# Two graph-network layers on one core: the score block in two PSUM tiles, and a new written-out order of all engines

## The chip, the core and the metric

The kernel runs on one core of a Trainium2 chip. The metric is device time in microseconds (us). A core has five engines that matter here, each with its own queue, which it works through in order: TensorE (PE: matrix products, with its weight loads shown as PEld), VectorE (DVE), ScalarE (ACT), GpSimd (POOL) and SyncE (SP), which here issues all transfers between HBM and the on-chip memory SBUF. TensorE writes its results to PSUM, a small memory of eight banks, from which DVE and ACT read; POOL works in SBUF alone.

## The reference

There are 64 graphs of 256 nodes with 256 features each, and for each graph an integer adjacency matrix. Two layers are applied one after the other; everything is float32. Cut to what matters:

```
# layer 0: 8 heads of 32; four relations r, of which this adjacency has values 0 and 1
q, k = x @ Wq + bq, x @ Wk + bk                    # split in heads
attn = softmax(q @ k.T / sqrt(32))
out  = sum over r of (attn * (adj == r)) @ (x @ Wv[r] + bv[r])
x    = layernorm(x + out @ Wo + bo)
x    = layernorm(x + gelu(x @ W1 + b1) @ W2 + b2)

# layer 1: 8 heads of 32
e    = leaky_relu(q @ k.T, 0.2)
attn = softmax(e where adj > 0, else -9e15)
h    = layernorm(attn @ v)
out  = layernorm(concat(h, x) @ Wffn.T) + x
```

## The kernel before

The function fast_path (line 232) treats graph after graph. For each one, program(g) (line 310) makes a list of operations, each with a name, the engine that runs it, and a function that emits its instructions. A name carries the layer and the group of four heads: q0, k0 and v0 are the queries, keys and values of layer 0; s01 is the score block of layer 0, head group 1; e and m are the exponentials (m the masked ones in layer 0, the positive part in layer 1); es is the sum of the two halves of e; po is the product with the values, with the row sums beside it; rd is the reciprocal of the row sums; o is their product; py is a transposition, y0, y1 and y2 are normalised rows; ph and pw2 are the two products of the feed-forward part; ph and pwa (without a number) belong to the end of layer 1. A suffix like /1 is the pair of heads inside a group, and #2 the second operation on the same name.

A score block (score, line 428) is eight matmuls of 32 rows: two halves of the keys, four heads each. Four heads use four strips of rows of the array at once. The products po (weighted, line 462) use four strips of columns at once. All other matmuls use the whole array. So TensorE changes between three forms: full array, row tiles (s) and column tiles (po).

All 1,024 scores per partition and pair of heads are read from PSUM twice. In layer 0, ACT takes exponentials (exps, line 443) and DVE adds a large negative number where the adjacency has an edge (without_edges, line 452); ACT then takes exponentials of that too, and POOL adds halves (halves_added, line 495). In layer 1, DVE adds the mask, ACT takes the positive part (emit_positive, line 704), POOL adds both (emit_leaky, line 708), and ACT takes exponentials of the sum.

PSUM is shared out by the table TAGS (line 58): "s" has one buffer of four banks, which holds a whole score block, and "g" has four buffers of one bank each for everything else, used in turn. When a tile has been read for the last time, its buffer can be written anew. Waits are put in by the framework from what reads and writes which tile. Buffers in SBUF are in the same table; e and m have three each.

The order is not left to the framework. in_order (line 45) gives each operation the time g x PERIOD + STARTS[name] and sorts all operations of all graphs by it; they are emitted in that order, so each engine's queue follows it. The times in STARTS (line 100) only rank; the period that the chip shows is another. The first four graphs and the last four have lists of their own, FIRST (line 120) and LAST (line 177), with one number for each operation. Graph 0 also has the fetches of the weights (fetch, line 510) and two small products, pbf and pmean (lines 553 and 564), which turn the last weight matrix wf into a scaled and centred one: pbf needs the operation "wide" (from the columns) and the fetched wf, then DVE copies and scales (emit_scaled, line 559), then pmean follows.

For one period in the middle of the run the order before is, on TensorE, with the graph relative to the newest one in brackets:

```
pk1[-2] pq1[-2] po00[-1] po01[-1] s10[-2] pv1[-2] pwo[-1] pwb[-2] pk0[0] pq0[0] py0[-1] s11[-2]
ph6 ph0 ph2 ph4[-1] s00[0] po10[-2] pw2 x8[-1] s01[0] po11[-2] pva0[0] pva1[0] py1[-1] ph[-2] pwa[-2]
```

At the start it begins pq0 pk0 pva1 s00 pbf pva0 pmean s01 po00 po01 pwo (all graph 0), then pq0 of graph 1, py0, pk0 of graph 1, ph0. SP issues adj, wq0, rows0, xT, wk0, wv01, cols, wo, wfT, rows1, x, wv1, w1, w2, wk1, wq1. At the end, with graph numbers, it is: py0.63, ph.63 x4, po10.62, pw2.63 x8, po11.62, ph.62, py1.63, pwa.62, pk1, pq1, s10, pwb, pv1, s11, po10, po11, ph, pwa (all of 63).

Of the kernel before, what the change touches and what calls it, by code (L numbers as in the profile page):

```python
# [17 lines left out]
ALPHA = 0.2  # L18
# [26 lines left out]
def in_order(programs, starts, period, first, last):  # L45
# [4 lines left out]
    for g, p in enumerate(programs):  # L50
# [31 lines left out]
    "s": ([HPG, NT, D], F32, 1),  # L82
# [18 lines left out]
    "xT": 16.39, "x": 17.62, "pk0": 18.03, "adj": 19.67, "neg": 20.08, "pq0": 21.31, "k0": 22.13, "q0": 25.00,  # L101
    "s00": 31.15, "m00/1": 33.61, "e00/0": 37.30, "e00/1": 38.52, "m00/1#2": 39.34, "m00/0": 40.16, "s01": 40.57,
    "e01/0": 40.98, "e01/1": 41.39, "m00/0#2": 44.26, "pva0": 45.49, "es01/1": 46.31, "v0/0": 46.72, "pva1": 47.13,
    "v0/1": 48.36, "es00/0": 48.77, "es00/1": 50.82, "m01/0": 52.05, "m01/0#2": 52.87, "m01/1": 54.92,
    "es01/0": 55.33, "m01/1#2": 57.38, "po00": 57.79, "rd00": 58.20, "po01": 58.61, "o0/0": 60.25,
    "DVE:po01": 61.48, "rd01": 62.30, "o0/1": 62.70, "pwo": 63.11, "DVE:po00": 63.52, "res": 64.34, "pwo#2": 65.57,
    "mv0": 66.80, "rs0": 67.21, "y0": 69.26, "py0": 71.72, "y0T": 72.54, "ph6": 75.41, "ph0": 76.64, "hT/6": 77.87,
    "ph2": 78.69, "hT/2": 79.10, "ph4": 79.51, "hT/0": 79.92, "hT/4": 80.74, "pw2": 81.97, "pw2#2": 82.38,
    "r1": 82.79, "r1#2": 83.20, "pw2#3": 84.43, "pw2#4": 84.84, "pw2#5": 85.66, "pw2#6": 86.07, "pw2#7": 86.48,
    "pw2#8": 88.93, "pw2#9": 91.80, "mv1": 93.03, "rs1": 93.44, "y1": 94.67, "py1": 97.54, "y1T": 97.95,  # L110
    "pk1": 100.00, "ACT:adj": 100.41, "pq1": 104.10, "q1": 104.51, "k1": 109.02, "s10": 109.43, "m10/0": 109.84,
    "pv1": 110.66, "v1": 111.07, "x2": 111.89, "pwb": 113.93, "e10/0": 114.75, "e10/1": 115.16, "e10/0#2": 115.98,
    "m10/1": 118.44, "e10/1#2": 118.85, "e10/0#3": 120.49, "es10/0": 120.90, "zb": 122.95, "s11": 123.36,
    "e11/1": 123.77, "x2#2": 124.18, "e11/0": 124.59, "e10/1#3": 125.82, "es10/1": 126.23, "m11/0": 127.05,
    "m11/1": 127.46, "e11/1#2": 128.28, "e11/0#2": 130.33, "po10": 131.56, "rd10": 134.02, "o1/0": 135.25,
    "e11/1#3": 136.89, "e11/0#3": 137.70, "es11/0": 138.11, "es11/1": 139.75, "po11": 142.21, "DVE:po10": 142.62,
    "rd11": 143.85, "o1/1": 145.08, "DVE:po11": 145.90, "ph": 149.18, "pwa": 149.59, "mv2": 151.23, "rs2": 151.64,
    "pwa#2": 152.46, "mv3": 153.28, "rs3": 153.69, "y2": 155.74, "y2#2": 156.15, "y2#3": 156.56, "SP:y2": 156.97,
# [3 lines left out]
        -2847.053, -2618.669, -2552.639, -2604.994, -2706.544, -2524.281, -2429.355, -2491.963, -2326.15, -2291.878,  # L122
        -2205.017, -2453.681, -2501.433, -2475.116, -1979.242, -2495.418, -2281.166, -2149.469, -1954.32, -1950.672,
        -2629.93, -2490.837, -2900.007, -2402.608, -1755.256, -2397.873, -2429.046, -2408.233, -2387.015, -2337.739,
        -2248.383, -2096.592, -2381.743, -2040.963, -2323.494, -1986.344, -2170.731, -2048.634, -1860.558, -2191.888,
        -2201.038, -2121.273, -1987.509, -1858.163, -1687.597, -1539.069, -1758.675, -1901.191, -1868.775, -1849.204,
        -1797.723, -1842.922, -1866.564, -1901.189, -1864.039, -1710.05, -1635.372, -1608.525, -1601.055, -1611.923,
        -1504.663, -1503.313, -1503.311, -1454.211, -1453.749, -1428.651, -1397.418, -1365.689, -1263.132, -1333.428,
        -1307.057, -1302.867, -1269.069, -1279.736, -1246.049, -1318.829, -1287.58, -1268.965, -1234.872, -1196.915,
        -1176.186, -1166.684, -1155.815, -1135.153, -1127.66, -1127.658, -1125.664, -1116.163, -1109.387, -1096.892,  # L130
        -1068.525, -1058.771, -834.708, -1034.909, -1034.369, -1037.42, -971.802, -873.683, -861.526, -817.316,
        -794.117, -948.046, -931.884, -938.676, -839.591, -800.872, -786.885, -935.815, -938.986, -873.329, -822.37,
        -800.254, -703.594, -628.579, -521.145, -703.592, -852.402, -753.92, -797.646, -753.918, -687.087, -549.142,
        -801.786, -794.56, -679.67, -651.382, -613.255, -519.88, -503.788, -460.172, -508.16, -452.842, -406.466,
        -405.026, -445.465, -387.29, -386.804, -373.855, -368.241, -277.528, -258.371, -211.016,
    ],
    [
        -1712.66, -1443.453, -1558.578, -1409.383, -424.973, -1332.342, -1515.918, -1376.199, -1389.201, -1376.896,
        -1176.315, -1175.399, -1171.179, -1142.744, -1372.605, -1177.435, -1233.494, -1225.381, -1169.756, -1364.499,
        -1211.174, -1210.635, -1283.409, -1142.483, -1107.236, -1024.81, -1042.32, -1168.101, -1163.006, -1109.044,  # L140
        -1086.417, -1040.287, -1117.876, -1135.775, -1092.749, -1107.742, -1028.857, -1019.047, -1019.045, -962.29,
        -953.415, -933.383, -905.03, -894.712, -878.269, -878.267, -878.265, -878.267, -829.154, -849.496, -805.626,
        -860.667, -839.105, -834.236, -762.88, -849.583, -795.469, -753.483, -652.438, -623.714, -612.52, -604.112,
        -604.11, -604.108, -597.853, -597.851, -580.455, -541.025, -525.23, -510.162, -510.16, -234.294, 26.726,
        -461.818, -418.06, -444.927, -353.251, -347.025, -276.942, -284.894, -256.944, -353.249, -292.158, -353.247,
        -288.969, -272.27, -239.253, -352.105, -312.477, -253.791, -237.655, -177.565, -140.907, -63.211, -56.41,
        -132.185, -252.617, -248.041, -236.522, -133.806, -99.059, -66.449, -235.239, -211.498, -143.046, -63.735,
        -23.871, -15.497, 7.986, 8.437, -15.495, 28.391, 37.806, 44.002, 37.535, 66.321, 66.323, 87.244, 87.246,
        116.225, 189.089, 204.842,
    ],  # L150
    [
        -1229.881, -526.973, -1181.68, -1178.71, 66.635, -396.146, -1031.055, -966.68, -943.117, -935.039, -608.969,
        -560.147, -579.485, -523.949, -808.47, -704.853, -753.672, -752.036, -617.846, -650.977, -671.842, -631.081,
        -641.14, -494.019, -442.274, -439.507, -456.199, -629.154, -609.944, -493.554, -466.947, -559.795, -577.488,
        -482.336, -418.455, -494.253, -414.141, -410.734, -406.722, -370.63, -396.854, -333.908, -310.914, -309.856,
        -309.854, -305.407, -305.13, -200.379, -114.553, -302.188, -284.917, -285.604, -156.698, -263.97, -217.918,
        -280.388, -230.946, -154.247, -111.16, -83.43, -79.414, -74.774, -71.445, -70.202, -70.114, -67.694, -67.692,
        -67.69, -53.693, -53.691, -53.689, -24.507, 209.443, 29.562, 64.838, -35.526, 9.223, 71.488, 99.662, 113.468,
        120.616, 69.818, 89.502, 70.022, 89.536, 110.394, 124.527, 109.105, 79.783, 120.842, 123.12, 124.465, 131.394,
        133.646, 137.555, 133.656, 123.327, 128.611, 127.875, 129.152, 133.924, 133.926, 123.329, 127.217, 128.709,  # L160
        133.424, 138.627, 142.388, 142.522, 146.364, 145.361, 151.44, 151.442, 153.783, 152.66, 153.785, 153.787,
        155.037, 155.83, 196.784, 209.445, 209.447,
    ],
    [
        -394.579, -455.288, -369.201, -318.002, -85.508, -1.925, -382.842, -372.891, -372.581, -353.322, -106.738,
        -80.656, -102.13, -71.463, -265.115, -179.435, -120.231, -102.022, -128.718, -168.609, -153.486, -32.837,
        -58.709, -10.119, 11.78, 27.092, 37.379, -119.809, -73.356, -86.43, -39.705, -50.805, -93.331, -55.921,
        -14.902, -55.763, 4.094, 33.398, 33.4, 47.121, 58.796, 65.314, 65.316, 67.626, 72.399, 72.484, 72.486, 72.401,
        78.893, 74.741, 81.291, 76.79, 81.396, 75.033, 81.051, 79.917, 81.961, 83.124, 83.126, 84.564, 85.156, 88.277,
# [62 lines left out]
def fast_path(nc, tc, a, out, bad):  # L232
# [13 lines left out]
    with ExitStack() as ctx:  # L246
# [63 lines left out]
        def program(g):  # L310
# [117 lines left out]
            def score(q, k, hg, n):  # L428
                def emit():
                    s, qT, kT = T(f"s{n}{hg}"), T(q), T(k)  # L430
                    for c in range(NT):
                        for j in range(HPG):
# [3 lines left out]
                                start=True, stop=True,  # L436
                            )

                op("PE", [q, k], [f"s{n}{hg}:s"], emit)
                for t in ("e", "m", "es"):  # L440
                    tags[f"{t}{n}{hg}"] = t

# [625 lines left out]
```

## Time and profile before

| what | value |
|---|---|
| median of three runs | 2937.29 us (2935.6 to 2937.31) |
| the profiled execution: own time | 2934.98 us |
| its span, first to last instruction | 2932.8 us |
| TensorE busy | 2882.9 us (98%) |
| DVE / ACT / POOL busy | 1961.4 / 1788.6 / 2017.2 us |
| granted clock of TensorE | 0.995 |
| DMA moved | 76.65 MB, mean 26 GB/s |
| one period in the middle (two successive po00) | 44.79 us |

A profile comes from one execution. The page gives busy time by engine, the span in 40 slices (a digit is the busy share in tenths), the chain of work that ended last, and groups of instructions. A line of the timeline has the start, the time up to the end of the last instruction, the engine, the line of the kernel, the operation, what it writes and reads, the array's form and the shape, and how many instructions were merged; in square brackets, the idle time before it and what ended it. One fp32 matmul is two instructions. The ends of matmuls are modelled, so starts are the safer thing to take differences of.

### The profile page before, as it was taken

To read this page: it belongs to the slowest core of one execution; us is meant where nothing else is said; L and a number is where in the kernel's file an instruction comes from. 1 tells how busy PE (TensorE), PEld (TensorE's weight loads), DVE (VectorE), ACT (ScalarE), POOL (GpSimd) and SP (SyncE) were. 2 spreads that over 40 slices of the span, in tenths; PEclk is the share of its full clock that TensorE was granted. 3 is DMA by queue.
4 is the path that set the end of the run, shared out by engine and by line. 5 is a ranking of instruction groups with operands and counts; after the bars stand their busy time and mean duration, and the time that the engine had idled before them with its cause. 6 is when DMAs were issued, how large, how long until landed. Compare 5 with 4: busy or idle time off the path is not lost.

```text
span 2932.8 us, 53746 instructions
## 1 busy us (share of the span) xinstructions
PE 2882.9 (98%) x21770; PEld 2154.7 (73%) x21770; DVE 1961.4 (67%) x3668; ACT 1788.6 (61%) x3009; POOL 2017.2 (69%) x1542
## 2 busy tenths in 40 slices
PE   7999999999999999999999999999999999999996
PEld 5777777777777777777777777777777777777774
DVE  4676676676766766766767667667667676676674
ACT  4656656566566566566665665665666656656653
POOL 2657767767767667677667676676776676766666
PEclk9999999999999999999999999999999999999997
DMA  3000100000000000000000000000000000010000
GB/s 123 15 19 16 33 30 15 30 19 26 30 15 30 30 15 30 30 15 30 21 24 30 16 30 30 16 30 30 15 30 23 23 30 16 30 34 15 30 16 8
DMA packets 74331, 76.65 MB, mean 26 GB/s; under 512 B 4448, under 2 KB 73568, under 8 KB 74080
## 3 DMA queue, kind: packets, MB, share of 16 engines
q1 hardware_dynamic: 74080, 73.17, 7.8%
q8 instruction: 174, 2.85, 0.4%
q14 instruction: 77, 0.63, 0.1%
HBM read 56.37 MB, written 16.78 MB: 25 GB/s over the span
## 4 chain that ended last, share of the span: by engine, by line
PE 96%; DVE 1%; POOL 1%; ACT 1%; issue 1%; DMA 0%; SPq 0%; DVEq 0%; ACTq 0%; POOLq 0%
PE ph L658 15%; PE pw L676 15%; PE po L470 12%; PE s L434 9%; PE pva L610 8%; PE pq L338 8%; PE pk L338 7%; PE pv L352 4%; PE pwa L352 4%; PE po L475 4%; PE pwo L352 4%; PE pwb L352 4%; PE py L364 2%; PE ph L364 1%; POOL e L710 1%
## 5 line engine op out<-in xcount | busy, mean ns | idle before, releaser
L710 POOL TENSOR_TENSOR e<-e,m 128x1024 f32<-128x1024 f32 x256 | 601.3, 2359 | 231.7 <-DVE e L457 148.8
L501 POOL TENSOR_TENSOR es<-e 128x512 f32<-128x512 f32 x512 | 644.4, 1274 | 153.1 <-ACT e L448 143.1
L457 DVE TENSOR_TENSOR m<-s,neg 128x1024 f32<-128x1024 f32 x256 | 311.8, 1219 | 483.8 <-PE s L434 327.7
L484 DVE RECIPROCAL rd<-po 128x256 f32<-128x256 f32 x256 | 449.2, 1755 | 132.1 <-PE po L475 124.5
L410 POOL TENSOR_TENSOR rs<-ve,neg_half 128x2 f32<-128x2 f32 x256 | 178.5, 697 | 479.6 <-DVE ve L405 479.3
L706 ACT ACTIVATE m<-s 128x1024 f32<-128x1024 f32 x256 | 255.2, 1022 | 371.2 <-PE s L434 226.1
L658 PE MATMUL ph<-y0T,w 128*128 128x256 f32 x2048 | 459.2, 382 | 0.7 <-ACT y0T L380 0.7
L676 PE MATMUL pw<-w,hT 128*128 128x256 f32 x2048 | 459.0, 382 | 0.0
L676 PEld LDWEIGHTS pw<-w,hT 128*128 128x128 f32 x2048 | 383.9, 190 | 75.6 <-issue 25.1
L658 PEld LDWEIGHTS ph<-y0T,w 128*128 128x128 f32 x2048 | 383.8, 190 | 71.2 <-issue 20.6
L457 DVE TENSOR_TENSOR e<-s,neg 128x1024 f32<-128x1024 f32 x256 | 302.1, 1218 | 146.8 <-PE s L434 122.9
L448 ACT ACTIVATE e<-s 128x1024 f32<-128x1024 f32 x256 | 258.9, 1014 | 187.4 <-PE s L434 167.1
L448 ACT ACTIVATE m<-m 128x1024 f32<-128x1024 f32 x256 | 269.5, 1055 | 66.8 <-DVE m L457 66.8
L434 PE MATMUL s<-q,k 32*128 32x256 f32 x4096 | 293.3, 400 | 3.1 <-DVE e L457 1.4
L448 ACT ACTIVATE e<-e 128x1024 f32<-128x1024 f32 x256 | 270.4, 1056 | 27.1 <-POOL e L710 26.2
L470 PE MATMUL po<-e,v 128*32 128x256 f32 x4096 | 276.4, 385 | 4.3 <-ACT e L448 4.3
L434 PEld LDWEIGHTS s<-q,k 32*128 32x128 f32 x4096 | 185.1, 184 | 89.9 <-issue 78.7
L610 PE MATMUL pva<-wv,xT 128*128 128x512 f32 x512 | 237.0, 605 | 0.0
L470 PEld LDWEIGHTS po<-e,v 128*32 128x32 f32 x4096 | 114.1, 109 | 125.5 <-issue 45.4
L665 ACT ACTIVATE hT<-ph,cols 128x256 f32<-128x256 f32 x512 | 194.6, 488 | 3.4 <-PE ph L658 2.6
L610 PEld LDWEIGHTS pva<-wv,xT 128*128 128x128 f32 x512 | 92.1, 189 | 115.7 <-issue 115.4
L475 PE MATMUL po<-es,ones 128*32 128x256 f32 x2048 | 160.2, 381 | 4.0 <-POOL es L501 4.0
(90 smaller groups left out, 4546.5 us busy)
## 6 DMA issues: line engine op xcount, KB each, us to landing
adj<-adjT_dram SPq DMA_DIRECT2D x64, 256.0 KB, 3.6
xT<-xT_dram SPq DMA_DIRECT2D x64, 256.0 KB, 3.0
x<-x_dram SPq DMA_DIRECT2D x64, 256.0 KB, 3.1
out_dram<-y SPq DMA_DIRECT2D x64, 256.0 KB, 2.2
w<-L_gnn_W_dram SPq DMA_DIRECT2D x2, 1024.0 KB, 10.3
rows<-rows_dram SPq DMA_DIRECT2D x1, 896.0 KB, 7.4
wv<-L_gnn_Wv_dram SPq DMA_DIRECT2D x3, 256.0 KB, 7.2
wq<-L_gnn_Wq_dram SPq DMA_DIRECT2D x2, 256.0 KB, 5.9
```

The lines of the kernel that those rows point to most:

```text
L338: nc.tensor.matmul(pt[:, o, :], lhsT=w[:, c, o * P : (o + 1) * P], rhs=s[:, c, :], start=(c == 0), stop=(c == KC - 1),)
L352: nc.tensor.matmul(pt[:, t, :], lhsT=T(s)[:, c, t * P : (t + 1) * P], rhs=w, start=(n == 0), stop=(n == len(parts) - 1),)
L434: nc.tensor.matmul(s[:, j, c, :], lhsT=kT[r, hg, c * P : (c + 1) * P], rhs=qT[r, hg, :], start=True, stop=True,)
L448: nc.scalar.activation(T(dst)[:, j], T(src)[:, j], AF.Exp, scale=scale, **kw)
L457: lambda: nc.vector.tensor_tensor(T(dst)[:, j], T(src)[:, j], T("neg")[:, None].to_broadcast([P, 2, NT, D]), ALU.add),
L470: nc.tensor.matmul(po[j * DH : (j + 1) * DH, 0, :], lhsT=v(c, j), rhs=T(e)[:, j, c, :], start=(n == 0 and c == 0), stop=(n == len(parts) - ...
L484: op("DVE", [po], [f"{rd}:rd"], lambda: nc.vector.reciprocal(T(rd), T(po)[:, 1, :]))
L501: lambda: on.tensor_tensor(T(dst)[:, j], T(e)[:, j, 0, :], T(e)[:, j, 1, :], ALU.add),
L610: nc.tensor.matmul(pv.rearrange("p r d -> p (r d)"), lhsT=s[:, c, t * P : (t + 1) * P], rhs=wv0[:, c].rearrange("p r d -> p (r d)"), start ...
L658: nc.tensor.matmul(ph[:, i, :], lhsT=w1[:, c, (f + i) * P : (f + i + 1) * P], rhs=s[:, c, :], start=(c == 0), stop=(c == KC - 1),)
L676: nc.tensor.matmul(T("pw2")[:, t, :], lhsT=T("hT")[:, f + i, t * P : (t + 1) * P], rhs=w2[:, f + i, :], start=(f + i == 0), stop=(f + i == ...
L710: nc.gpsimd.tensor_tensor(T(f"e1{hg}")[:, j], T(f"e1{hg}")[:, j], T(f"m1{hg}")[:, j], ALU.add)
```

## The change

There are two parts. First, the score block is split: the tag "s" now has tiles of half the size and two of them, so a block has one tile for each pair of heads, and each reader names the tile of its pair. The eight matmuls are the same, in the same order, and write to one tile or the other. PSUM as a whole is used as before (two tiles of two banks in place of one of four).

Second, the tables STARTS, FIRST and LAST are new.

```diff
-    "s": ([HPG, NT, D], F32, 1),
+    "s": ([2, NT, D], F32, 2),
...
 def score
-                    s, qT, kT = T(f"s{n}{hg}"), T(q), T(k)
+                    s, qT, kT = [T(f"s{n}{hg}{pair}") for pair in range(2)], T(q), T(k)
                     for c in range(NT):
                         for j in range(HPG):
                             r = slice(j * DH, (j + 1) * DH)
                             nc.tensor.matmul(
-                                s[:, j, c, :], lhsT=kT[r, hg, c * P : (c + 1) * P], rhs=qT[r, hg, :],
+                                s[j // 2][:, j % 2, c, :], lhsT=kT[r, hg, c * P : (c + 1) * P], rhs=qT[r, hg, :],
                                 start=True, stop=True,
                             )
-                op("PE", [q, k], [f"s{n}{hg}:s"], emit)
+                op("PE", [q, k], [f"s{n}{hg}{pair}:s" for pair in range(2)], emit)
...
 def exps
-                    nc.scalar.activation(T(dst)[:, j], T(src)[:, j], AF.Exp, scale=scale, **kw)
-                op("ACT", [src if src.startswith("s") else f"{src}/{pair}"], [f"{dst}/{pair}"], emit)
+                    s = T(dst)[:, j] if src == dst else T(src)
+                    nc.scalar.activation(T(dst)[:, j], s, AF.Exp, scale=scale, **kw)
+                op("ACT", [f"{dst}/{pair}" if src == dst else src], [f"{dst}/{pair}"], emit)
...
 def without_edges
-                        T(dst)[:, j], T(src)[:, j], T("neg")[:, None].to_broadcast([P, 2, NT, D]), ALU.add
+                        T(dst)[:, j], T(src), T("neg")[:, None].to_broadcast([P, 2, NT, D]), ALU.add
...
-                    exps(f"s0{hg}", f"e0{hg}", SCALE, pair, 2 * hg + pair)
-                    without_edges(f"s0{hg}", f"m0{hg}", pair)
+                    exps(f"s0{hg}{pair}", f"e0{hg}", SCALE, pair, 2 * hg + pair)
+                    without_edges(f"s0{hg}{pair}", f"m0{hg}", pair)
...
-                    without_edges(f"s1{hg}", f"e1{hg}", pair)
+                    without_edges(f"s1{hg}{pair}", f"e1{hg}", pair)
-                        nc.scalar.activation(T(f"m1{hg}")[:, j], T(f"s1{hg}")[:, j], AF.Relu, scale=1.0 / ALPHA - 1.0)
+                        nc.scalar.activation(T(f"m1{hg}")[:, j], T(f"s1{hg}{pair}"), AF.Relu, scale=1.0 / ALPHA - 1.0)
-                    op("ACT", [f"s1{hg}"], [f"m1{hg}/{pair}"], emit_positive)
+                    op("ACT", [f"s1{hg}{pair}"], [f"m1{hg}/{pair}"], emit_positive)
```

The new STARTS (the old ones follow from the order shown above):

```diff
+    "xT": 47.54, "adj": 54.92, "neg": 55.74, "pq0": 56.97, "q0": 60.25, "pk0": 70.08, "k0": 70.90, "s000": 72.95,
+    "e00/0": 81.15, "m00/1": 81.56, "m00/0": 87.70, "e00/1": 90.98, "pva0": 93.44, "s010": 94.26, "v0/0": 95.08,
+    "e01/0": 96.72, "x": 97.13, "m00/1#2": 97.95, "pva1": 100.82, "res": 101.64, "e01/1": 102.05, "es00/1": 102.87,
+    "v0/1": 103.28, "es01/0": 104.10, "m00/0#2": 106.56, "m01/1": 107.38, "m01/1#2": 107.79, "m01/0": 108.61,
+    "m01/0#2": 109.43, "es00/0": 111.07, "po00": 111.48, "rd00": 112.30, "o0/0": 112.70, "es01/1": 113.11,
+    "po01": 114.34, "rd01": 114.75, "o0/1": 115.16, "DVE:po01": 115.57, "DVE:po00": 116.39, "ACT:adj": 118.44,
+    "pwo": 118.85, "pwo#2": 119.26, "mv0": 119.67, "rs0": 123.77, "y0": 124.18, "py0": 124.59, "y0T": 125.00,
+    "r1": 129.51, "ph0": 131.97, "ph4": 132.79, "hT/0": 134.43, "hT/4": 134.84, "ph2": 135.25, "hT/2": 135.66,
+    "ph6": 136.07, "hT/6": 136.48, "r1#2": 138.11, "pw2": 138.52, "pw2#2": 138.93, "pw2#3": 139.34, "pw2#4": 139.75,
+    "pw2#5": 140.16, "pw2#6": 140.57, "pw2#7": 141.39, "pw2#8": 141.80, "pw2#9": 142.21, "mv1": 142.62,
+    "rs1": 145.49, "y1": 145.90, "py1": 148.36, "y1T": 148.77, "pk1": 153.69, "pq1": 154.51, "k1": 155.33,
+    "q1": 158.20, "s100": 159.02, "e10/0": 159.84, "m10/0": 160.66, "e10/1": 161.89, "x2": 163.52, "m10/1": 163.93,
+    "s110": 165.98, "e11/0": 166.80, "m11/1": 167.21, "pv1": 167.62, "v1": 168.03, "m11/0": 170.49,
+    "e10/1#2": 171.31, "e11/1": 172.13, "pwb": 172.54, "e10/0#2": 173.36, "e11/0#2": 175.41, "zb": 176.64,
+    "e10/1#3": 177.05, "es10/1": 177.46, "e11/1#2": 182.38, "e10/0#3": 183.20, "e11/0#3": 183.61, "es10/0": 184.02,
+    "e11/1#3": 186.89, "es11/1": 193.03, "po10": 193.85, "es11/0": 194.67, "po11": 196.31, "rd10": 199.18,
+    "DVE:po11": 199.59, "o1/0": 200.00, "DVE:po10": 200.41, "rd11": 201.23, "o1/1": 202.46, "x2#2": 206.15,
+    "ph": 221.72, "mv2": 225.82, "rs2": 226.23, "pwa": 227.87, "pwa#2": 228.28, "mv3": 228.69, "rs3": 229.10,
+    "y2": 229.92, "y2#2": 230.33, "y2#3": 230.74, "SP:y2": 237.30,
...
```

Sorted, one period on TensorE now reads:

```
pva1[-1] pk1[-2] pq1[-2] pq0[0] s10[-2] po00[-1] po01[-1] s11[-2] pv1[-2] pwo[-1] pk0[0] ph[-3] pwb[-2] s00[0]
py0[-1] pwa[-3] ph0 ph4 ph2 ph6[-1] pw2 x8[-1] pva0[0] po10[-2] s01[0] po11[-2] py1[-1]
```

A graph's operations are now spread over some four periods where they took three, and the end of layer 1 (ph, pwa) runs one period later. FIRST and LAST (numbers left out) give these orders. At the start TensorE's queue is pbf pmean pq0 pk0 s00 pva1 s01 pva0 po00 po01 pwo (graph 0), pk0 and pq0 of graph 1, py0, s00 of graph 1, ph0 ph2 ph6 ph4, pw2 x8, pva1 and pva0 of graph 1, py1, s01 of graph 1, pk1. SP issues cols, wv01, wk0, xT, wfT, wq0, rows1, adj, rows0, x, w1, wv1, wo, wk1, w2, wq1. At the end: pwo.63, pwb.62, pv1.62, py0.63, pwa.61, ph0.63, ph4, ph2, the first pw2, ph6, the other seven pw2, po10.62, po11.62, py1.63, pq1, pk1, ph.62, s10.63, pv1.63, pwa.62, s11.63, pwb, po10, po11, ph, pwa (all of 63). There POOL has rs3.62, y2.62 and their like behind the last half sum es11/1.63, and DVE has y2.62 between o1/0.63 and rd11.63.

## The prediction

> **What bounds the kernel now.** I read the page first: which engine is full, and where it is not.
>
> ```profile
> span 2932.8 us, 53746 instructions
> ...
> PE 2882.9 (98%) x21770; PEld 2154.7 (73%) x21770; DVE 1961.4 (67%) x3668; ACT 1788.6 (61%) x3009; POOL 2017.2 (69%) x1542
> ...
> PE   7999999999999999999999999999999999999996
> ...
> PEclk9999999999999999999999999999999999999997
> ```
>
> TensorE is full in 38 slices of 40; only the first and last (73.3 us each) have room. Cut to 300-2700 us, the table of waits has no wait of TensorE at all. But a busy record is no proof of a full array: ends are modelled. So I went to the timeline of TensorE and took differences of starts over one period:
>
> ```profile
> 1411.65 1.89 PE L338 MATMUL pk<-y1T,wk 128*128 128x256 f32 x8
> 1413.37 1.89 PE L338 MATMUL pq<-y1T,wq 128*128 128x256 f32 x8
> 1415.19 1.07 PE L470 MATMUL po<-e,v 128*32 128x256 f32 x16
> ...
> 1419.65 1.15 PE L434 MATMUL s<-q,k 32*128 32x256 f32 x16
> 1420.72 1.99 PE L352 MATMUL pv<-wv,y1T 128*128 128x256 f32 x8
> 1422.55 1.89 PE L352 MATMUL pwo<-wo,o 128*128 128x256 f32 x8
> 1424.28 1.89 PE L352 MATMUL pwb<-wf,y1T 128*128 128x256 f32 x8
> ...
> 1459.98 1.07 PE L470 MATMUL po<-e,v 128*32 128x256 f32 x16
> ```
>
> A graph takes 1459.98 - 1415.19 = 44.79 us. Eight full-array matmuls take 1.73 us between full-array neighbours (pk to pq, pwo to pwb). They take 1.82 ahead of po (pq) and 1.83 behind s (pv). That 0.1 us is the cost of changing the array's form; nothing waits there. Single starts in the trace give it in ns: full-array matmuls start 216 apart, the last before a change 309 (+93), the first after one 320 (+104). Groups of four row-tile matmuls start 196 apart, the first 300 (+104), the last 304 (+108); column-tile groups 220 (+24) and 309 (+113).
>
> At the ends TensorE does wait. The start (timeline of TensorE):
>
> ```profile
> 8.85 3.75 PE L338 MATMUL pq<-xT,wq 128*128 128x256 f32 x8 [8.85 <-DMA xT<-xT_dram]
> ...
> 22.83 1.10 PE L566 MATMUL pmean<-wf,mean_w 128*128 128x256 f32 x4 [1.73 <-DVE wf L562]
> ...
> 36.74 1.99 PE L352 MATMUL pwo<-wo,o 128*128 128x256 f32 x8 [3.00 <-DVE o L487]
> ...
> 42.25 0.90 PE L364 MATMUL py<-ident,y 128*128 128x128 f32 x4 [1.80 <-DVE y L416]
> ```
>
> The last score block, graph 63, layer 1 (timelines of PE, DVE, ACT, POOL):
>
> ```profile
> 2894.00 1.15 PE L434 MATMUL s<-q,k 32*128 32x256 f32 x16 [0.68 <-ACT q L506]
> ...
> 2895.21 1.23 DVE L457 TENSOR_TENSOR e<-s,neg 128x1024 f32<-128x1024 f32 x1 [1.20 <-PE s L434]
> ...
> 2896.53 1.94 ACT L706 ACTIVATE m<-s 128x1024 f32<-128x1024 f32 x2 [2.58 <-DVE e L457]
> ...
> 2898.50 1.23 DVE L457 TENSOR_TENSOR e<-s,neg 128x1024 f32<-128x1024 f32 x1 [2.06 <-ACT m L706]
> ...
> 2898.54 4.66 POOL L710 TENSOR_TENSOR e<-e,m 128x1024 f32<-128x1024 f32 x2 [1.84 <-ACT m L706]
> ```
>
> ACT reads the other pair of heads than DVE does, in other banks, and still starts only when DVE ends: readers of one PSUM tile go in turn.
>
> **What the Trainium skill says.** "TensorEngine Tiling (Array Packing)", Key Properties: changing the tiling mode drains TensorE. The trace agrees: 117 to 217 ns a change. "PSUM — Partial Sum Buffer", PSUM bank collisions raise a hardware error: engines must be kept apart by bank and quadrant, ScalarE against VectorE reads included. The turn-taking above is wider than that, by tile, so two tiles free what two banks already allowed. "Perfetto Trace Analysis", Identifying the Most-Contended Engine: TensorE's busy share does not measure headroom. Agreed: the 0.2 us of a change is inside "busy".
>
> **The change part by part.** *Changes of form.* No matmul is added or removed. Merging both orders from the tables and counting neighbours on TensorE: full-array work is left for tiled work 259 times before (191 to row tiles, 68 to column tiles) and 200 after (139 + 61), and entered as often; column-tile blocks are entered from another form 192 times before, 186 after; row-tile blocks 256 times in both. All six kinds of neighbour occur before already (the rarest 65 times), so no price is unknown: 59 x (93 + 104) = 11.62 us, 6 x (24 + 113) = 0.82 us, together 12.4 us less. A steady graph has four visits to tiles before (po00 po01 s10; s11; s00 po10; s01 po11) and three after (s10 po00 po01 s11; s00; po10 s01 po11), so one full exit and one entry go: period 44.79 - 0.20 = 44.59 us.
>
> *The steady order must stay free of waits.* I laid the new order out over one period, pva1 at 0: pk1 1.7, pq1 3.5, pq0 5.2, s10 7.0, po00 8.1, po01 10.3, s11 12.5, pv1 13.6, pwo 15.4, pk0 17.2, pwb 19.3, s00 21.1, py0 22.2, pwa 22.8, ph 24.5, pw2 31.4, pva0 38.3, po10 40.1, s01 41.6, po11 42.6, py1 44.1. Against it I set each queue with measured durations (without-edges 1.22, reciprocal 1.75, exp 1.0-1.1, leaky add 2.36, half sums 1.27). The tightest:
> - s10 at 7.00 needs q1. ACT: k1 starts 1.93 after pk1 (as in the trace) at 3.65, two exponentials of 0.96, q1 0.58: done 6.63, plus 0.06 to PE: 0.3 us spare. The second exponential starts at 5.09 and needs DVE's m01/1, done at 4.6, behind rd11 and v0/1.
> - pk1 at 46.3 needs y1T, done 45.7: 0.6. pwo needs o0/1 (po01's end 12.4 + 0.2 + 1.75 + 0.42 = 14.8): 0.6. s00's second tile needs e11/1 (pwo's end 17.2 + 0.2 + 0.7 + 1.1 + 1.2 = 20.4): 0.7. py0 needs y0: 0.9. PSUM's four small buffers: pq1 takes po11's, free at 2.8: 0.6.
> So no wait. Busy per period is 30.5 us on DVE, 27.9 on ACT, 31.5 on POOL: none becomes the bound. xT and adj are issued a period ahead (3.0 and 3.6 us to land): covered.
>
> *Two tiles.* In the steady part they cost and bring nothing: no PE wait exists to remove; same matmuls, same reads. At the ends they let DVE and ACT read in parallel.
>
> *Start.* SP's order puts wfT fifth (before: ninth), xT stays fourth, wq0 goes from second to sixth, adj from first to eighth; pbf and pmean now lead TensorE's queue, so pq0 and everything behind wait for wfT. 1.55 MB are issued up to it; before, the 1.41 MB up to wk landed at 2.71 + 6.7 = 9.4 us, the 1.66 MB up to the first wv at 10.3. So pbf at about 9.9; I bound it below by 7.5, for the case that the slow early landings came from the 384 KB of broadcast rows, now ninth. What moved back (adj, rows, x) comes within 3.6 MB; before, x landed after 3.84 MB at 8.73 + 7.3 = 16.0, and s00 will not run before 18: covered. Then pbf 1.0, copy and scale 1.2, pmean 1.1: pq0 at 10.7-13.1 (before 8.85). In return the middle loses pbf 1.0, the wait 1.73 and pmean 1.1 = 3.8. k0's latency is no longer covered by pva1 (+1). Followed on: pwo at 35-37 (before 36.74), py0's wait is filled with pk0 and pq0 of graph 1, later y1 and y0 of graphs 0 and 1 are waited for (0.6 + 0.8). Sum: -2.4 to 0; I take -1.
>
> *End.* po10 of graph 62 moves behind pw2: 0.86 + 0.43 = 1.3 us of work out of the stretch that ends with pw2. From pw2's end to s10 of graph 63 before: 2881.15 to 2894.00 = 12.85, with y1 behind a reciprocal (py1 at +4.95) and pwa ahead of pk1. After: y1 runs directly (add, stats, rs, y = 0.2 + 0.7 + 1.1 + 0.8 + 1.0: py1 at +3.85), y1T +1.7, pq1 and pk1 3.5, k1 0.8: s10 at +9.9; 3.0 saved. From s10 on POOL sets the pace: four leaky adds and four half sums, 14.3 us, began 4.54 after s10; with DVE and ACT on different tiles they begin at 1.2 + 1.22 + 1.22 = 3.7: 0.85 saved. But rs3 of graph 62 now stands behind them on POOL, y2 waits for it on DVE, and rd11, o1/1 stand behind y2: 0.6 back. Waits for o0/1, y0 (about 1.5) replace 1.64 before. End: -1.3 - 3.0 - 0.25 - 0.1 = -4.6, plus or minus 2.
>
> Sum: -12.4 - 1 - 4.6 = -18.0. Span 2932.8 to 2914.8; the profiled execution's own time 2934.98 (2.2 outside the span) to 2917.0; the runs' median, 2.3 above that, to 2919.3.
>
> **The rivals.** *Slower: s10 waits for q1.* If two exponentials and q1 on ACT run later than laid out, by rd11 on DVE slipping behind a late po11 for instance, the 0.3 us are gone, and each 0.1 us of wait a graph costs 6.4 us. From 18.0/64 = 0.28 us of wait the kernel is slower; at 0.6, 2919 + 38 = 2957. For it: a tight spot with an in-order queue of four behind it. Against: all durations in the layout are measured ones, and the other queues are idle a third of the period. At 0.2 us, 2932: no change.
> *Only the middle gains.* The start loses 4 (wfT even later), the end's new queue positions eat its gain: 2937.3 - 12.4 + 4 = 2929.
> *The changes of form are free*, their 0.2 us being absorbed elsewhere: then only the ends move, 2932. Against: the same step has the same length in every steady graph, to about 1 ns, whatever the other engines do then.
>
> **How the numbers follow.** Main case 0.76, own range 2913 to 2926 (start -2.4 to 0, end -2.6 to -6.6, the waits unseen). Middle only 0.08. No change (0.2 us of wait, or free changes) 0.06. Slower 0.10. Within 0.2% (5.9 us) is about what cannot be told from no change. Faster 0.84, same 0.06, slower 0.10; 2912 to 2932 leaves out the slower case and about a tenth of the rest.
>
> **What would show it.** Right: period 44.59 in the timeline, three visits, no PE wait at s10; the full-array steps of 309 and 320 ns, four each a graph, become three each; pbf first at 7.5-10 us; ACT and DVE on s at once after the last score block. Wrong: a row "PE s <- ACT q" or "PE s <- DVE e" in the waits of 300-2700 us, a period above 44.79, or graph 1's first ph starting after 90 us (84.96 before).

## The result, and the profile after

The changed kernel takes 2904.41 us (median of four runs, 2903.45 to 2904.93), the kernel before in the same comparison 2936.44 (2934.96 to 2937.31). The ratio is 0.9891, with a 95% interval of 0.9874 to 0.9908. The prediction was 2919 us with a range of 2912 to 2932: the direction is right, the gain is nearly twice the forecast one, and the time lies outside the range.

The profiled execution has an own time of 2903.45 us. These are the lines of its page that answer to those of the page before:

```profile
span 2901.5 us, 53555 instructions
PE 2863.8 (99%) x21770; PEld 2152.2 (74%) x21770; DVE 1964.0 (68%) x3668; ACT 1776.7 (61%) x3011; POOL 2008.1 (69%) x1542
PEclk9999999999999999999999999999999999999998
```

The span is 31.3 us shorter with the same 21,770 matmul instructions; busy time of TensorE fell by 19.1 us although no matmul went. As the prediction noted, a change of the array's form hides inside "busy".

One period in the middle, from the timeline of TensorE after (start, duration, engine, line, operation):

```profile
1402.20 1.15 PE L439 MATMUL s<-q,k 32*128 32x256 f32 x16
...
1408.81 1.99 PE L357 MATMUL pv<-wv,y1T 128*128 128x256 f32 x8
1410.63 1.89 PE L357 MATMUL pwo<-wo,o 128*128 128x256 f32 x8
1412.36 1.89 PE L343 MATMUL pk<-xT,wk 128*128 128x256 f32 x8
1414.09 0.60 PE L369 MATMUL ph<-ident,o 128*128 128x128 f32 x4
1414.53 1.89 PE L357 MATMUL pwb<-wf,y1T 128*128 128x256 f32 x8
...
1417.42 0.66 PE L369 MATMUL py<-ident,y 128*128 128x128 f32 x4
1417.92 1.89 PE L357 MATMUL pwa<-wf,o 128*128 128x256 f32 x8
...
1446.70 1.15 PE L439 MATMUL s<-q,k 32*128 32x256 f32 x16
```

The first and last line are s10 of two graphs that follow each other: 44.50 us, against 44.79 before and 44.59 predicted. There is no wait of TensorE between 90 and 2830 us. Note two differences. pv, behind a score block, takes 1410.63 - 1408.81 = 1.82 us to the next start, and pwo, behind a full-array product, 1.73: entering costs 0.09 here, as the prediction has it. But py, a transposition of 128 columns behind a score block, takes 0.50, and ph, the same behind a full-array product, 0.44: there entering costs only 0.06.

The start, from the same view; pbf now leads the queue:

```profile
9.67 2.05 PE L562 MATMUL pbf<-wf,wide 128*128 128x256 f32 x4 [9.67 <-DMA wf<-WffnT_dram]
...
14.37 3.38 PE L343 MATMUL pq<-xT,wq 128*128 128x256 f32 x8
```

The last graph's first score block, from the timelines of PE, DVE, ACT and POOL:

```profile
2863.39 1.15 PE L439 MATMUL s<-q,k 32*128 32x256 f32 x16 [0.24 <-ACT k L513]
...
2864.57 2.40 DVE L464 TENSOR_TENSOR e<-s,neg 128x1024 f32<-128x1024 f32 x2 [0.21 <-PE s L439]
2864.69 2.16 ACT L713 ACTIVATE m<-s 128x1024 f32<-128x1024 f32 x2 [1.35 <-PE s L439]
...
2867.05 7.02 POOL L717 TENSOR_TENSOR e<-e,m 128x1024 f32<-128x1024 f32 x3 [1.92 <-DVE e L464]
```

DVE and ACT now read side by side, each on its own tile, and POOL's first leaky add starts 3.66 us after the block (4.54 before).

**Where the time went.** I priced every operation of TensorE at the start-to-start interval that its matmuls have between neighbours of their own form, added the measured prices of the changes of form (leaving full-array work 93 ns, entering it 104, or 56 where a transposition enters; row tiles 104 and 108, column tiles 24 and 113), and took the rest of the span as waiting. Time in which the matmuls themselves run slowly is therefore in the rows of waiting too. It lies at the ends: the first matmuls of a run take about twice their later time, and near the end the clock is low for stretches (in the profile after, the granted clock was 0.50 from 2874.3 to 2888.0 us).

| us | before | after | difference | predicted |
|---|---|---|---|---|
| changes of form | 131.4 | 113.3 | -18.1 | -12.4 |
| waiting up to the first pw2 of graph 1 | 23.7 | 21.9 | -1.8 | -1 |
| from there to the first pw2 of graph 62 | 5.9 | 0.7 | -5.3 | 0 |
| from there to the end of the span | 35.2 | 29.1 | -6.2 | -4.6 |
| sum | | | -31.3 | -18.0 |

The row predicted with 0 holds waits of the kernel before that the prediction had passed over. Three of them, from its timeline of TensorE:

```profile
156.95 1.99 PE L352 MATMUL pwa<-wf,o 128*128 128x256 f32 x8 [1.03 <-DVE v L618]
...
238.59 1.15 PE L434 MATMUL s<-q,k 32*128 32x256 f32 x16 [0.54 <-DVE m L457]
...
2757.62 2.02 PE L338 MATMUL pq<-y1T,wq 128*128 128x256 f32 x8 [2.26 <-ACT y1T L380]
```

They lie in graphs 2 to 5 and 60 to 62, where the hand-made first and last orders meet the steady one. The prediction had cut its table of waits to 300-2700 us, and its sums for the start and the end leave these waits out.

The longest of them is a matter of turns at the score tile. ACT's timeline before, and then y1T of the same graph with two tiles and the old order (the first experiment below):

```profile
2756.00 1.02 ACT L448 ACTIVATE e<-s 128x1024 f32<-128x1024 f32 x1 [7.07 <-DVE m L457]
...
2757.01 1.01 ACT L380 ACTIVATE y1T<-py,cols 128x256 f32<-128x256 f32 x2
```

```profile
2749.81 1.02 ACT L380 ACTIVATE y1T<-py,cols 128x256 f32<-128x256 f32 x2 [3.33 <-PE py L364]
```

Before, an exponential of the second pair of heads stands in ACT's queue until DVE has read the first pair from the same tile, y1T stands behind it, and pq on TensorE behind that. With two tiles y1T waits only for its own input.

### The profile page after: what moved, and what is told of

Its sections match the earlier page's. It is cut to its first block, busy times and chain, and to the rows that moved or that the text cites. A ratio compares the mean times of both kernels' runs of the same rounds, so it can differ in the third digit from the quotient of the medians.

```text
span 2901.5 us, 53555 instructions
## 1 busy us (share of the span) xinstructions
PE 2863.8 (99%) x21770; PEld 2152.2 (74%) x21770; DVE 1964.0 (68%) x3668; ACT 1776.7 (61%) x3011; POOL 2008.1 (69%) x1542
## 4 chain that ended last, share of the span: by engine, by line
PE 97%; DVE 1%; POOL 1%; issue 1%; DMA 0%; ACT 0%; SPq 0%; DVEq 0%; POOLq 0%
PE ph L665 15%; PE pw L683 15%; PE po L477 12%; PE s L439 9%; PE pq L343 8%; PE pk L343 8%; PE pva L617 7%; PE pv L357 4%; PE pwa L357 4%; PE pwo L357 4%; PE po L482 4%; PE pwb L357 4%; PE py L369 3%; PE ph L369 1%; POOL e L717 0%
## 5 line engine op out<-in xcount | busy, mean ns | idle before, releaser
L665 PE MATMUL ph<-y0T,w 128*128 128x256 f32 x2048 | 452.9, 379 | 0.0
L683 PE MATMUL pw<-w,hT 128*128 128x256 f32 x2048 | 452.7, 379 | 0.0
L397 DVE TENSOR_TENSOR pw<-pw,r 128x512 f32<-128x512 f32 x64 | 44.8, 700 | 471.8 <-PE pw L683 464.3
L464 DVE TENSOR_TENSOR m<-s,neg 128x1024 f32<-128x1024 f32 x256 | 301.0, 1213 | 37.4 <-ACT e L455 23.5
L385 ACT ACTIVATE y0T<-py,cols 128x256 f32<-128x256 f32 x128 | 65.2, 559 | 182.4 <-PE py L369 182.3
```

The lines of the kernel that those rows point to most:

```text
L464: lambda: nc.vector.tensor_tensor(T(dst)[:, j], T(src), T("neg")[:, None].to_broadcast([P, 2, NT, D]), ALU.add),
L665: nc.tensor.matmul(ph[:, i, :], lhsT=w1[:, c, (f + i) * P : (f + i + 1) * P], rhs=s[:, c, :], start=(c == 0), stop=(c == KC - 1),)
L683: nc.tensor.matmul(T("pw2")[:, t, :], lhsT=T("hT")[:, f + i, t * P : (t + 1) * P], rhs=w2[:, f + i, :], start=(f + i == 0), stop=(f + i == ...
```

## The experiments

Ten measurements, in three groups (four, four and two rows), each group on one chip with its own runs of the kernel before. All times are medians. Where a row of the first group is compared with the kernel after, that is the 2904.41 us of the result above.

| kernel | us | before, same group | ratio | 95% interval |
|---|---|---|---|---|
| two tiles, order of before | 2925.71 | 2936.82 | 0.9959 | 0.9945 to 0.9973 |
| one tile, order of after | 2991.01 | 2936.82 | 1.0181 | 1.0164 to 1.0198 |
| four visits | 2916.43 | 2936.82 | 0.9930 | 0.9914 to 0.9947 |
| ph behind s11 | 2904.10 | 2936.82 | 0.9888 | 0.9872 to 0.9905 |
| after, again | 2903.50 | 2935.39 | 0.9890 | 0.9874 to 0.9907 |
| later start | 2895.70 | 2935.39 | 0.9864 | 0.9848 to 0.9881 |
| half sums on DVE at the end | 2905.35 | 2935.39 | 0.9898 | 0.9881 to 0.9914 |
| these three together | 2895.28 | 2935.39 | 0.9865 | 0.9848 to 0.9881 |
| later start, again | 2895.44 | 2935.91 | 0.9862 | 0.9846 to 0.9879 |
| later start and ph | 2894.30 | 2935.91 | 0.9858 | 0.9842 to 0.9875 |

### Two tiles with the order of before

```diff
-STARTS, FIRST, LAST                        # the tables of after
+STARTS, FIRST, LAST                        # the tables of before, "s00" now named "s000" and so on
```

> Two tiles for a score block, but the three order tables of the kernel before. Theory A (the prediction's step: in the middle the two tiles bring nothing, since TensorE has no wait there to remove): period of a graph 44.79 us as before, only the ends gain 0 to 4 us, total 2932 to 2936 us. Rival B (the tiles themselves bring a good part of the 32 us): period under 44.79 or total under 2925 us.

Measured: 2925.71 us, 11.1 less than before in the same group (8.7 in the spans of the two profiles; its runs lie between 2922.6 and 2927.2). That is between the two theories. The period is untouched: po00 of two neighbouring graphs starts at 1411.77 and 1456.56, 44.79 us apart. The waiting falls in three places: by 0.8 us up to graph 1, by 5.6 us between graphs 1 and 62 (from 5.9 to 0.3), and by 2.3 us at the end, of which 1.1 is a low clock in the profile of before. So the split alone removes what the junctions of the orders cost in the kernel before, while every queue keeps its order; for DVE and ACT all that changed is that they need not take turns on one tile. TensorE, for its part, may write the first tile as soon as its own pair has been read (in the profile after, the block at 23.75 us writes its first two matmuls and then waits 0.43 us for DVE); the two effects were not tried apart, but the ACT lines above show the first at work. That the steady middle would not change was expected; the size was not: the end and start were counted, the junctions were not.

### One tile with the order of after

```diff
-    "s": ([2, NT, D], F32, 2),
+    "s": ([HPG, NT, D], F32, 1),
```

and the readers index the pair inside the tile again, as before.

> The new order tables, but one PSUM tile of four banks for a score block as before, so that its four readers go in turn. Theory A (the tiles bring nothing in the middle): period 44.50 us as in the changed kernel, total 2904 to 2910 us. Rival B (the order with s11 only 5.5 us behind s10 needs the parallel reading): the four reads of s10 in turn take 4 x 1.2 us from 1.2 us after its start, end 0.3 to 0.5 us after s11's turn on TensorE, so TensorE waits at s11 in every graph: period 44.8 to 45.0 us, total 2920 to 2935 us, and a row of waits of s for DVE or ACT of 15 to 30 us.

Measured: 2991.01 us, 1.8% slower than before and 87 us above after. Even the rival, which had 15 to 30 us of waiting, was too mild, and it looked for the wait at s11, where only the smaller part is. The period is 45.77 us (1405.21 to 1450.98). TensorE's waits between 300 and 2600 us (engine, what it waited for, total, times, longest), and the timelines of PE, ACT and DVE around one of them:

```profile
PE s L439 <- DVE e L465: 43.0, 50, 0.9
PE s L439 <- ACT m L714: 13.4, 51, 0.3
```

```profile
1412.34 1.02 ACT L714 ACTIVATE m<-s 128x1024 f32<-128x1024 f32 x1
1413.39 1.23 DVE L465 TENSOR_TENSOR e<-s,neg 128x1024 f32<-128x1024 f32 x1 [1.44 <-ACT m L714]
1414.77 1.15 PE L439 MATMUL s<-q,k 32*128 32x256 f32 x16 [0.86 <-DVE e L465]
```

The last line is s00, which waits 0.86 us because the four readers of s11 pass through the tile one after another: ACT, then DVE, which had itself waited 1.44 us for ACT. With s11 waiting for s10's readers as well (0.26 us at 1405.21), a graph loses 1.27 us. That is 43.0 + 13.4 = 56.4 us over some 51 graphs, or 1.1 us in each, and the rest of the 1.27 is spread thinner. So the new order can't live on one tile. All four combinations side by side: before 2936.8, split alone 2925.7, order alone 2991.0, both 2904.4. The effects of the two parts do not add: the order gains only where the tile is split.

### Back to four visits

Only one number is changed: pv1 moves ahead of s11, so that the tiled work before and after it is two visits again.

```diff
-    "s110": 165.98, ... "pv1": 167.62,
+    "s110": 165.98, ... "pv1": 165.97,
```

> The changed kernel with pv1 moved ahead of s11 in the middle 56 graphs, so s11 is a visit of its own again: one more exit from full-array work (93 ns) and one more entry (104 ns) a graph. Theory (changes of form cost what the steps show): period 44.50 + 0.197 = 44.69 to 44.70 us, total 2904.4 + 56 x 0.197 = 2915 us (2913 to 2917). Rival (they cost nothing by themselves and the gain came from elsewhere): 2903 to 2907 us.

Measured: 2916.43 us, 12.0 above after (11.6 when each is set against its own kernel before). The period is 1452.28 - 1407.58 = 44.70 us: 0.20 more, which is the 93 + 104 ns of one full exit and one entry. Over 56 graphs that is 11.0 us. In the profile another 1.7 us are lost in the last graph, where pq and pk ran at a clock of 0.50 (2871 to 2874 us; the last section comes back to it). There is no new wait in the middle. The price of a change of form is thus measured with a single operation moved, and a rival in which it is free falls.

### ph behind s11

ph, a transposition, goes from between two full-array products to directly behind s11, so that it is the one that enters from tiles rather than pv.

```diff
-    "ph": 221.72, "mv2": 225.82,
+    "ph": 217.40, "mv2": 217.41,
```

> The changed kernel with the transposition ph of layer 1 moved from behind pk0 to directly behind s11 (and the statistics mv2 that read it moved ahead of pwo#2 on DVE), in the middle 56 graphs: the third and last entry from tiles into full-array work is now a transposition too. Theory (a transposition as the first full-array work costs 56 ns of entry instead of 104): period 44.50 - 0.05 = 44.45 us, total 2904.4 - 2.7 = 2901.7 us. Rival 1 (the cheaper entry belongs to py's place and not to transpositions): 44.50 us, 2904 us. Rival 2 (mv2 earlier on DVE makes y0 or e11/1 late): a wait of TensorE appears and the period is over 44.50.

Measured: the period falls to 1445.26 - 1400.81 = 44.45 us, 0.05 less, as 104 - 56 ns say. The time does not: 2904.10 us. Near the end, where the moved ph meets the last orders, pwo waits 0.84 us for DVE at 2699.65, and the score block at 2747.63 takes 1.96 us instead of 1.15, because its second tile's reader on DVE stands behind mv2, which waited for the moved ph. In the account used above, changes of form fall by 2.6 us and waiting up to graph 62 grows by 2.7: all that the middle gained.

### After again, a later start, and half sums on DVE

The three share a chip. In the first, nothing is changed.

> The changed kernel once more, as the measure for the three that follow on the same chip: 2904 us, within 2 us.

Measured: 2903.50 us (2903.09 to 2903.75), 0.9 below the first measurement.

In the second, pbf and pmean leave the head of TensorE's queue, and SP issues in the order in which the first graph needs things:

```diff
+MOVES = [
+    ('xT', 0, 'behind', 'c_cols', 0), ('c_wq0', 0, 'behind', 'xT', 0), ('c_wk0', 0, 'behind', 'c_wq0', 0),
...
+    ('pbf', 0, 'ahead', 'pwo', 0), ('c_scaled', 0, 'behind', 'pbf', 0),
+    ('pmean', 0, 'ahead', 'py0', 0), ('c_wf', 0, 'behind', 'pmean', 0),
...
+        for name, g, place, name2, g2 in MOVES:
+            at = {(o.name, o.g): o for o in ordered}
+            o = at[name, g]
+            ordered.remove(o)
+            ordered.insert(ordered.index(at[name2, g2]) + (place == "behind"), o)
```

> The changed kernel with another start: SP issues cols, xT, wq0, wk0, adj, wv01, rows0, x first and wfT tenth; pbf moves from the head of TensorE's queue to just ahead of pwo of graph 0 and pmean to just ahead of py0, with their DVE work behind them. Theory (everything at the start waits behind pbf for wfT): pq0 starts at 5 to 7 us in place of 14.4, pwo of graph 0 4 to 6 us earlier, the total 3 to 5 us less than the changed kernel. Rival (the start is bound by the chain through exponentials, reciprocals and normalisation, whichever load comes first): under 1 us less.

Measured: 2895.70 us, 7.8 below after. From the timeline of TensorE:

```profile
5.38 3.75 PE L373 MATMUL pq<-xT,wq 128*128 128x256 f32 x8 [5.38 <-DMA wq<-L_gnn_Wq_dram]
...
24.75 1.13 PE L592 MATMUL pbf<-wf,wide 128*128 128x256 f32 x4
25.72 0.59 PE L387 MATMUL pwo<-wo,o 128*128 128x256 f32 x2
27.78 1.56 PE L387 MATMUL pwo<-wo,o 128*128 128x256 f32 x6 [1.46 <-DVE o L524]
```

pq0 starts at 5.38 instead of 14.37, and pbf fills 0.97 us in front of a wait that is there anyway. Waiting up to graph 1 falls from 21.8 to 13.8 us. Two things changed: xT and wq0, all that pq0 needs, now come first, and pq0 no longer stands behind pbf, which waited 9.67 us for wf. How much each brings was not tried apart. The expectation (3 to 5) had the direction and about half the size.

In the third, graph 63's half sums of layer 1 go from POOL, which sets the pace there, to DVE, with rd10 and o1/0 moved ahead:

```diff
-                    halves_added("POOL", f"e1{hg}", f"es1{hg}", pair)
+                    halves_added("DVE" if g == B - 1 else "POOL", f"e1{hg}", f"es1{hg}", pair)
...
+    ('rd10', 63, 'ahead', 'es11/1', 63), ('DVE:po10', 63, 'behind', 'rd10', 63),
+    ('o1/0', 63, 'behind', 'DVE:po10', 63), ('y2', 62, 'behind', 'o1/1', 63),
```

> The changed kernel with the four half sums es of layer 1 of graph 63 on DVE in place of POOL, and rd10, its flags and o1/0 moved ahead of the last of them, y2 of graph 62 moved behind o1/1. Theory (behind the last score block POOL sets the pace with 4 x 2.34 + 4 x 1.25 = 14.3 us): the stretch from s10 of graph 63 to the end becomes 2 to 4 us shorter than 38.1 us. Rival (the end hangs on the DVE chain of reciprocals, which only gets longer): no shorter, or up to 2 us longer.

Measured: 2905.35 us, 1.9 above after; a miss for the idea. The timelines of POOL and DVE, and at the end a line of PE, show why:

```profile
2869.17 4.71 POOL L725 TENSOR_TENSOR e<-e,m 128x1024 f32<-128x1024 f32 x2
2872.53 1.90 DVE L516 TENSOR_TENSOR es<-e 128x512 f32<-128x512 f32 x1 [2.19 <-ACT e L463]
...
2875.49 0.68 DVE L516 TENSOR_TENSOR es<-e 128x512 f32<-128x512 f32 x1
2875.64 2.75 POOL L725 TENSOR_TENSOR e<-e,m 128x1024 f32<-128x1024 f32 x1 [1.76 <-DVE e L472]
2876.09 0.68 DVE L405 TENSOR_TENSOR zb<-pwb,bf 128x512 f32<-128x512 f32 x1
2876.69 2.25 DVE L516 TENSOR_TENSOR es<-e 128x512 f32<-128x512 f32 x1
...
2882.19 0.68 DVE L516 TENSOR_TENSOR es<-e 128x512 f32<-128x512 f32 x1
...
2882.93 1.07 PE L490 MATMUL po<-es,ones 128*32 128x256 f32 x4 [1.37 <-DVE es L516]
```

A half sum takes DVE 0.68 us when POOL is idle at its start, and 1.90 and 2.25 us when a leaky add is running. The zb between them has the same size but one input in PSUM, and takes 0.68 us while the add is running. The ends tell more: the adds end at 2869.17 + 4.71 = 2873.88 and 2875.64 + 2.75 = 2878.39, the two slow half sums at 2874.43 and 2878.94, each 0.55 us later. The Trainium skill says this in "SBUF — State Buffer", Who interferes with whom: a VectorE instruction with two SBUF inputs contends with a GpSimd instruction that reads SBUF, and contention is an exclusive lock. The trace agrees, and in the other direction too: the add that starts at 2875.64, while a half sum runs, takes 2.75 us where the mean is 2.36.

The delay reaches the end through DVE's queue. The edit puts rd10 and o1/0 ahead of the last half sum. Behind the slowed half sums rd10 starts at 2879.93 us instead of 2878.01 in after, the last half sum follows at 2882.19, TensorE's row sums wait 1.37 us for it, and rd11 starts at 2884.05 instead of 2882.97. POOL's wait of 1.76 us costs nothing by itself: freed of its half sums, POOL ends the last add at 2878.39, against 2878.84 in after. How much of the loss is the contention and how much the moved order was not tried apart.

Then the three edits together (ph moved in graphs up to 55 only, away from the last orders):

> The new start, the new end, and ph behind s11 (with mv2 ahead of pwo#2) in graphs 4 to 55 only, so that the order of the last graphs is the changed kernel's. Theory (three independent terms that add): 4 + 3 + 52 x 0.048 = 9.5 us less than the changed kernel, 2895 us (2892 to 2898). Rival (the wait seen where ph's new place meets the last orders comes back, or start and end interact): 2898 to 2902 us.

Measured: 2895.28 us. The start keeps its 8 us, the middle gains 2.5 us in changes of form, and waiting behind the last s10 grows by 2.0 us (27.8 against 25.8). There is no wait where the middle meets the last orders now. The total is the expected one, but by luck: the start brought 8 us instead of 4, and the half sums cost 2 instead of bringing 3.

### The later start and ph

The same without the half sums on DVE, and beside it the later start alone once more.

```diff
+MIDDLE = {"ph": 217.40, "mv2": 217.41}
...
-        at = edge or [starts[o.name] for o in p]
+        at = edge or [MIDDLE[o.name] if o.name in MIDDLE and g < 56 else starts[o.name] for o in p]
```

> The later start alone, once more, for the comparison on one chip: 2895.7 within 1.

> The kernel after with the later start (pbf just ahead of the first pwo, pmean just ahead of the first py0, the transfers in the order of need) and with ph moved from ahead of pwb to directly behind s11 in the 56 graphs from 4 to 59 or fewer (up to graph 55), the end being that of the kernel after. If the gains of the two moves add where nothing is changed at the end: start -8.0 and period 44.50 to 44.45 over some 50 graphs, -2.4: 2895.7 - 2.5 = 2893.2. Rival: the middle's gain is again eaten where the last graphs' orders begin, as in the two runs before with ph moved: 2895.7, and waits of TensorE beyond 2600 us that the run with the later start alone does not have.

Measured: 2895.44 us (2895.05 to 2895.89) for the start alone, 2894.30 (2894.07 to 2895.18) with ph: 1.1 us less, where 2.5 were expected; the two ranges just overlap. It is the lowest median of all. No new wait shows up: the transposition py1 of the last graph starts at 2846.65 against 2848.73, 2.1 us earlier. Then pq and pk of layer 1 run slowly in the profiled execution, which is also the slowest of its four. From the view of stretches of its trace (busy time of PE, PEld, DVE, ACT and POOL, then the granted clock):

```profile
2848.00:2851.00 3.00, 2.70 (x8) 2.16 (x9) 2.97 (x3) 0.71 (x2) 0.39 (x1) 0.69 0.00 0
2851.00:2854.00 3.00, 3.00 (x13) 2.40 (x12) 0.77 (x3) 0.81 (x2) 0.00 (x0) 0.74 0.00 0
```

The clocks of 0.69 and 0.74 are means of 3 us: the granted clock stood at 0.50 from 2849.2 to 2852.6 us, and the two products lose 1.7 us by it. In the run beside it they run at 1.00. So the expected gain is there until 2848 us, and what this execution shows behind that is the clock, not an eaten gain. Whether the other three executions lost the same there I can't say; their times are 0.7 to 1.1 us below the profiled one.

## Why the prediction was right and wrong

**The direction and the mechanism of the middle were right.** One visit to the tiles fewer per graph saves 0.20 us. Going back to four visits costs just that, with one operation moved and no wait added. (Two readings are loose, without harm to the sums: the prediction's "eight matmuls" are eight instructions, and its 196 ns between groups of four run from the last start of one group to the first of the next; from first to first it is 216.) The laid-out order ran without waits: s10, the slower rival's place, does not wait for q1 in any middle graph, and pk1, pwo, py0 and the second tile of s00 keep their room.

**The step that failed first is "all six kinds of neighbour occur before already, so no price is unknown".** A kind of neighbour was taken too coarsely. Entering full-array work was priced at 104 ns, whatever enters. In the new order two of the three entries of a graph are a transposition: py0 behind s00, py1 behind po11. Entering there costs 56 ns. Before, 5 of 259 entries were of that sort; after, 123 of 200. The price could be read before, in the two of the five that have no wait beside them; this is one, from the timeline of TensorE before:

```profile
2797.03 1.15 PE L434 MATMUL s<-q,k 32*128 32x256 f32 x16
2798.11 0.66 PE L364 MATMUL py<-ident,y 128*128 128x128 f32 x4
2798.60 1.88 PE L610 MATMUL pva<-wv,xT 128*128 128x512 f32 x4
```

py takes 0.49 us to the next start here, and 0.44 behind full-array work. So 118 entries more at 48 ns less: 5.7 us, the difference of 18.1 and 12.4. In a period it is 2 x 0.048 = 0.10, and 44.79 - 0.20 - 0.10 = 44.49 against 44.50 measured. The run with ph behind s11 shows the same 0.05 on its own. The sum had the right mechanism; this term of it was mis-sized. Why a transposition enters more cheaply stays open: a product of 512 columns (pva) enters at 104 ns like one of 256, so the price does not simply grow with the width (533 ns to the next start in the trace before, 429 between its like).

**The second is "in the steady part they cost and bring nothing", of the two tiles.** In the exact middle of the kernel before that holds: its period with two tiles stays 44.79. But the sentence was stretched over everything between the first and last score block. In graphs 2 to 5 and 60 to 62 the kernel before waits 5.6 us, and the split alone takes these waits away. And the new order needs the split: with one tile it loses 1.27 us in every graph. The layout of the period in the prediction had the readers' durations, but used them as if the two tiles were there without asking what it would be without.

**The start** was sized about right (-1.8 against -1, within -2.4 to 0): pbf came at 9.67 (9.9 forecast), pq0 at 14.37 instead of the 10.7 to 13.1 expected, because the first matmuls of a run are slow (the prediction's own line for pq0 at the start shows 3.75 us for eight instructions that take 1.89 later; pbf takes 2.05 us at the head of the queue and 1.13 us in the later start; it was priced at 1.0, and pmean, 1.87 to the next start, at 1.1); pwo at 33.82 in place of 35 to 37 gave that back, so the good total is two misses that offset each other. What the prediction did not see is how much lay there: the later start is worth 8 us more.

**The end** came out at -6.2 against -4.6, plus or minus 2. From the end of pw2 to s10 of the last graph it is 2863.39 - 2853.84 = 9.55 us (9.9 forecast, 12.85 before); but some 1.1 us of those 12.85 were a low clock (0.63 and 0.52 in 2885-2889 us), not waiting, as the split alone with the same order shows: 11.59. That part of the gain is luck. The leaky adds begin 3.66 after s10, as forecast (3.7). rs3 behind the half sums costs 0.1 to 0.2, not 0.6: y2 runs at 2882.05, and rd11, which stands behind it, at 2882.97, when po11 is only just done.

Of the 13.3 us by which the span was missed, 5.7 are the transpositions, 5.3 the junctions, 1.6 the end (of which about 1.1 the clock) and 0.8 the start. The range of 2912 to 2932 let the start and end vary and held fixed the two terms that were mis-sized: the price of entering, and the 0 of the two tiles between the ends.

**The rivals** fell: no wait at s10, the ends did gain, and the changes of form are not free.

## What to carry to other kernels

Price a change of state by what comes next as well as by what went before, and look for the pairing in the old trace that matches the new one exactly. Before writing that a resource brings nothing, read the waits of the whole run, the junctions of hand-made orders included, and ask whether the new order could run without the resource. When two edits come together, run each alone: here one was worth 11 us, the other cost 54, and both gave 32.

## What the runs showed of the hardware that was not expected

- Entering full-array work from tiles costs 104 ns in front of a product of 256 or 512 columns and 56 ns in front of a transposition of 128.
- A half sum on DVE takes 0.68 us alone and 1.90 to 2.25 us beside a running add on POOL, ending 0.55 us after it; an operation of the same size with one input in PSUM is not slowed.
- TensorE's clock can fall where TensorE waits only briefly. "TensorE: Matmul & The Clock Gate" of the Trainium skill, Part 1, puts the idle window at about 3.4 us. Ahead of pq and pk of the last graph, all ten profiles with the new order have two waits of 0.65 to 0.68 us and no longer wait near them. Behind them the granted clock stood at 0.50 for one stretch of 3.4 us in three (2849.2 to 2852.6 us in the later start and ph, 2870.8 to 2874.2 in four visits, 2946.7 to 2950.1 with one tile), and at 1.00 in the other seven. Short waits spread over a graph did not bring it down: with one tile TensorE waits 0.26 and 0.86 us in a graph of the middle, and the clock is 1.00 from 45.4 to 2946.6 us. What decides is not shown. It costs 1.7 us in each of the first two, as much as many an edit at this level, so a difference of 1 us between two profiles should be looked for in the clock first.
